# Layer 1's first buffers at the other end of SBUF beside the transform back, one pool of PSUM banks for both, the weights' sums and the first units' loads moved

## The chip, the cores and the metric

One core of a Trainium2 chip. The time is that of one execution on the device, in microseconds (us); lower is better. The kernel before runs in 5853.41 us, the median of three executions (5851.69 to 5869.86).

The engines are called by the profile's names: PE (matrix multiplications; PEld is its weight load), DVE (vector), ACT (scalar, with activation tables), POOL (GpSimd) and SP (SyncE, which here only issues DMAs). SBUF is the on-chip memory, PSUM the eight banks in which PE accumulates.

## The reference

The input x is (16, 16, 256, 256) in float32: 16 batches of 16 channels of 256 x 256 points. Two layers follow each other, each a group norm (8 groups of 2 channels in a batch), a branch and a residual sum.

```python
x = x + _L0_conv_ref(_gn(x), ty, tx, poles1, poles2, residues)
x = x + _L1_conv_ref(_gn(x), W1, b1, Wred, bred, Wspan, bspan, W2, b2, Weca)
```

Layer 0 takes a two-dimensional Fourier transform, multiplies it by a kernel given by poles and residues, and goes back: `x1` is the inverse transform and `x2` the sum over the poles, and `x1 + x2 / Nx / Ny` is added to x.

Layer 1 works on each channel as a picture of its own: a 3x3 convolution to four features with Mish; the bottom half of the rows is reduced to one channel and gives the kernel of a 3x3 involution of the top half; top and bottom are concatenated with the channels of the bottom rolled by one, a 3x3 convolution over 64 channels with Mish follows, and its mean over the picture gives a gate for each channel that multiplies the layer's input.

## The kernel before

It is one program of four stages: `layer0_forward`, `layer0_mix`, `layer0_back` and `layer1`. The change is in the last two and in the seam between them.

**The transform back (`layer0_back`, about 2262 to 2915 us).** It goes over 256 channels (16 batches of 16), four channels to a group, so 64 groups. `fetch` issues a group's loads on SP: two loads of h from `hd` in DRAM (512 KB each, e = 0 and 1), and one of x (1 MB). For each channel PE adds up `py` in a bank, alternating `iy` times h (L951) and f times `e2` (L952), and for each pair of channels it makes `pf` (L940); ACT copies `odd` and `f` to SBUF; DVE makes `o` (L962, L963); POOL adds it to x (L964); DVE takes the moments `st` (L968). For each group `norm` follows one group behind: `mv` on DVE (L976), `gn_mean` on PE (L34), four small operations on DVE, `gn_var` on PE (L42), a square root on ACT between small DVE operations (`gnr`, L46), then the normed `zb`, one half on DVE and one on POOL (L983), and two stores of `zb` to `zn` in DRAM on SP (L992). `zn` has a border of zeros; its first and last row come from a tile `zero` (memset L903, stores L905 on POOL).

The h that the first groups read was stored to `hd` by the stage before (`hd<-h`, L788, issued by POOL).

PSUM in the back: two banks for pf, four for py, one for gn_mean and gn_var together.

**Layer 1 (`layer1`, from about 2919 us).** It has 144 units, nine for each batch. A unit loads its z rows from `zn` (`load_rows`, eight loads on SP, L1115), and then does the first convolution `c` (L1144, two turns of 48 passes), Mish into `bot` (L1153) and `wide` (L1161), the reduction `pr` (L1172) to `r` (L1182), the involution `pd` (L1194, 192 passes) with `t` and `top` on DVE (L1209, L1211), and stores to `cf`. The second convolution (`c2ps`, L1272) of the batch before is interleaved. While unit i is in its involution, unit i+1's convolution stands in front of it in PE's order: c(0), pr(0), c(1), pd(0), pr(1), c(2) and so on.

Before the first unit come the loads of the weights (L58, L1066), sums of them on DVE (L1054 to L1071), `mean2` and `std2` from the norms' scalars (L1081, L1082), memsets on POOL (`zero1`, the two `wide`, borders), and the load of ACT's Mish table (`preload_act_table_set`).

**What sets the order.** In both stages the order on PE, ACT, DVE and POOL is that of the program's text inside `tc.manual_schedule`. The order on SP is set by the framework's scheduler. Tile pools hand out their buffers in turn, and a buffer's next user waits for the last reader. A pool that is opened where a closed pool lay waits for that pool's last users; this holds for all of layer 1's pools in the kernel before, since the back's pools close when `layer0_back` returns. At most eight of the DMAs that SP issues are under way at once, by the program's semaphores.

The order of the back, for each channel n:

```python
for n in range(C * nb + 5):
    if n and n % 4 == 0 and n <= C * nb:
        fetch(n // 4 + 2)
    if n < C * nb:
        channel(n)
        if n % 2 == 0:
            rows_poles(n + 2)
    if 1 <= n <= C * nb:
        moments(n - 1)
    if n and n % 4 == 0 and n <= C * nb:
        last = norm(n // 4 - 1)
    next(last, None)
```

Of the kernel before, what the change touches and what calls it, by code (L numbers as in the profile page):

```python
# [1 line left out]

# [8 lines left out]
F32 = mybir.dt.float32  # L11
# [7 lines left out]
C = 16  # L19
N = 256  # L20
# [9 lines left out]
def group_norm_scalars(nc, sm, psum, ones, mv, n, neg_mean, rstd, times=1.0):  # L30


    mean = psum.tile([P, n], F32, tag="gn", name="gn_mean")
# [7 lines left out]
    var = psum.tile([P, n], F32, tag="gn", name="gn_var")  # L41
# [30 lines left out]
def layer0_forward(ctx, tc, d, al, bd, tabs):  # L72
# [36 lines left out]
    psn = ctx.enter_context(tc.tile_pool(name="psn", bufs=1, space=PSUM))  # L109
    passing = ExitStack()  # L110
# [65 lines left out]
    def halves(b, cg, eo, mv):  # L176
# [5 lines left out]
        yield from group_norm_scalars(nc, sm, psn, ones, mv, 2, nm, rs, 4.0)  # L182
# [694 lines left out]
@with_exitstack  # L877
def layer0_back(ctx, tc, d, hd, bd, zn, mr, ed):

    nc = tc.nc
    nb = d["x"].shape[0]
    cp = ctx.enter_context(tc.tile_pool(name="bc", bufs=1))
    iy = load(nc, cp, d["iy"], [P, 2, P], "iy")
    ones = load(nc, cp, d["ones"], [P, P], "ones")


    e1 = cp.tile([P, C, N], F32, name="e1")
    e2 = cp.tile([P, C, N], F32, name="e2")  # L890
    for k in range(0, C, 4):
        for i, t in enumerate((e1, e2)):
            nc.sync.dma_start(out=t[:, k : k + 4], in_=ed[:, i, k : k + 4])

    hp = ctx.enter_context(tc.tile_pool(name="bh", bufs=4))
    fp = ctx.enter_context(tc.tile_pool(name="bf", bufs=3))
    sm = ctx.enter_context(tc.tile_pool(name="bs", bufs=3))
    psf = ctx.enter_context(tc.tile_pool(name="psf", bufs=2, space=PSUM))
    psy = ctx.enter_context(tc.tile_pool(name="psy", bufs=4, space=PSUM))
    psn = ctx.enter_context(tc.tile_pool(name="psn", bufs=1, space=PSUM))  # L900

    zero = cp.tile([nb, C * (N + 2)], F32, name="zero")
    nc.gpsimd.memset(zero, 0.0)  # L903
    for y in (0, N + 1):
        nc.gpsimd.dma_start(out=zn[:, y].rearrange("b c x -> b (c x)"), in_=zero)  # L905
    zbuf = [cp.tile([P, 2, 4, N + 2], F32, name=f"zb{i}") for i in range(3)]
    for t in zbuf:
        for x in (0, N + 1):
            nc.gpsimd.memset(t[:, :, :, x : x + 1], 0.0)

    groups, r2s, fs = {}, {}, {}

    def fetch(i):

        if i >= 4 * nb:
            return
        b, k0 = i // 4, i % 4 * 4
        if k0 == 0:
            r2s[b] = fp.tile([P, P], F32, tag="r2", name="r2")
            nc.sync.dma_start(out=r2s[b], in_=bd[b])  # L920
        h = hp.tile([P, 2, 4, N], F32, tag="h", name="h", bufs=3)
        for e in range(2):
            nc.sync.dma_start(
                out=h[:, e].rearrange("p k x -> p (k x)"),
                in_=hd[e, :, :, b % 2, b // 2, k0 : k0 + 4].rearrange("v f k x -> (v f) (k x)"),
            )
        x = hp.tile([P, 4, 2, N], F32, tag="x", name="x")
        nc.sync.dma_start(
            out=x.rearrange("p k h x -> p (k h) x"),
            in_=d["x"][b, k0 : k0 + 4].rearrange("k (h p) x -> p (k h) x", p=P),  # L930
        )
        groups[i] = h, x, sm.tile([P, 4, 6], F32, tag="st", name="st")

    def rows_poles(n):

        if n >= C * nb:
            return
        b, k = divmod(n, C)
        pf = psf.tile([P, 2, N], F32, tag="pf", name="pf")
        nc.tensor.matmul(pf, lhsT=r2s[b], rhs=e1[:, k : k + 2], start=True, stop=True)  # L940
        fs[n] = fs[n + 1] = fp.tile([P, 2, N], F32, tag="f", name="f")
        nc.scalar.copy(fs[n], pf)

    def channel(n):

        k = n % C
        h, x, _ = groups[n // 4]
        f = fs.pop(n)
        py = psy.tile([P, 2, N], F32, tag="py", name="py")
        for e in range(2):  # L950
            nc.tensor.matmul(py[:, e], lhsT=iy[:, e], rhs=h[:, e, k % 4], start=True, stop=False)  # L951
            nc.tensor.matmul(  # L952
                py[:, e],
                lhsT=f[:, k % 2, P * e : P * e + P],
                rhs=e2[:, k],
                start=False,
                stop=True,
            )
        odd = fp.tile([P, N], F32, tag="odd", name="odd")
        nc.scalar.copy(odd, py[:, 1])  # L960
        o = fp.tile([P, 2, N], F32, tag="o", name="o")
        nc.vector.tensor_tensor(o[:, 0], py[:, 0], odd, ALU.add)  # L962
        nc.vector.tensor_tensor(o[:, 1], py[:, 0], odd, ALU.subtract)  # L963
        nc.gpsimd.tensor_tensor(x[:, k % 4], x[:, k % 4], o, ALU.add)  # L964

    def moments(n):
        _, x, st = groups[n // 4]
        nc.vector.bn_stats(st[:, n % 4], x[:, n % 4].rearrange("p h x -> p (h x)"))  # L968

    def norm(i):  # L970

        b, k0 = i // 4, i % 4 * 4
        _, x, st = groups.pop(i)
        mv = sm.tile([P, 2, 2], F32, tag="mv", name="mv")
        for g in range(2):
            nc.vector.bn_aggr(mv[:, g], st[:, 2 * g : 2 * g + 2].rearrange("p c s -> p (c s)"))  # L976
        yield
        g0 = k0 // 2
        nm, rs = mr[:, b, g0 : g0 + 2, 0], mr[:, b, g0 : g0 + 2, 1]
        yield from group_norm_scalars(nc, sm, psn, ones, mv, 2, nm, rs)  # L980
        z = zbuf[i % 3]
        for g, eng in ((0, nc.vector), (1, nc.gpsimd)):
            eng.tensor_scalar(  # L983
                z[:, :, 2 * g : 2 * g + 2, 1 : N + 1],
                x[:, 2 * g : 2 * g + 2].rearrange("p k h x -> p h k x"),
                nm[:, g : g + 1],
                rs[:, g : g + 1],
                ALU.add,
                ALU.mult,
            )  # L990
        for h in range(2):
            nc.sync.dma_start(  # L992
                out=zn[b, 1 + P * h : 1 + P * h + P, k0 : k0 + 4].rearrange("p k x -> p (k x)"),
                in_=z[:, h].rearrange("p k x -> p (k x)"),
            )
        yield

    E = mybir.EngineType  # L1000
    with tc.manual_schedule(engines={E.PE, E.Activation, E.DVE, E.Pool}):
        for i in range(3):
            fetch(i)
        rows_poles(0)
        last = iter(())
        for n in range(C * nb + 5):
            if n and n % 4 == 0 and n <= C * nb:
                fetch(n // 4 + 2)
            if n < C * nb:
                channel(n)  # L1010
                if n % 2 == 0:
                    rows_poles(n + 2)
            if 1 <= n <= C * nb:
                moments(n - 1)
            if n and n % 4 == 0 and n <= C * nb:
                last = norm(n // 4 - 1)
            next(last, None)

# [3 lines left out]
def layer1(ctx, tc, d, zn, cf, mr, nb):  # L1024
# [9 lines left out]
    wp = ctx.enter_context(tc.tile_pool(name="l1w", bufs=1))  # L1034
    zp = ctx.enter_context(tc.tile_pool(name="l1z", bufs=3))
    fp = ctx.enter_context(tc.tile_pool(name="l1f", bufs=2))
    rp = ctx.enter_context(tc.tile_pool(name="l1r", bufs=3))
    op = ctx.enter_context(tc.tile_pool(name="l1o", bufs=4))
    sm = ctx.enter_context(tc.tile_pool(name="l1s", bufs=2))
# [5 lines left out]
    nc.scalar.preload_act_table_set("mish")  # L1045
# [7 lines left out]
    w02 = wp.tile([P, 2, 32], F32, name="w02")  # L1053
    nc.vector.tensor_tensor(w02, c2[:, :, 0], c2[:, :, 2], ALU.add)  # L1054
    halves = []
    for name, op_ in (("w_sum", ALU.add), ("w_difference", ALU.subtract)):
        w = wp.tile([P, 2, 32], F32, name=name)
        nc.vector.tensor_tensor(w, w02, c2[:, :, 1], op_)
        nc.vector.tensor_scalar(w, w, 0.5, None, ALU.mult)
        halves.append(w)  # L1060
    weights = [c2[:, :, 0], *halves, c2[:, :, 2]]
    w12 = wp.tile([P, 2, 32], F32, name="w12")
    nc.vector.tensor_tensor(w12, c2[:, :, 1], c2[:, :, 2], ALU.add)
    pm = load(nc, wp, d["pm"], [P, 3, C], "pm")
    weca = wp.tile([P, 3], F32, name="weca")
    nc.sync.dma_start(out=weca, in_=d["weca"].to_broadcast([P, 3]))  # L1066

    wca = wp.tile([P, C], F32, name="wca")
    nc.vector.tensor_scalar(wca, pm[:, 0], weca[:, 0:1], None, ALU.mult)
    for k in (1, 2):  # L1070
        nc.vector.scalar_tensor_tensor(  # L1071
            wca, pm[:, k], weca[:, k : k + 1], wca, ALU.mult, ALU.add
        )
# [551 lines left out]
```

## Time and profile before

| | |
|---|---|
| median of three executions | 5853.41 us (5851.69, 5853.41, 5869.86) |
| the profiled execution's own time | 5856.29 us |
| its span (first to last instruction) | 5854.5 us |
| mean granted clock of PE | 0.982 of full |
| busy share of the span | PE 93%, DVE 80%, ACT 40%, POOL 49% |
| DMA | 1370 MB, mean 234 GB/s |
| chain of waits by engine | PE 69%, DVE 17%, DMA 8%, issue 4% |
| last ph matmul of the mix, first py of the back | 2262.6 us, 2281.09 us |
| last py of the back | 2905.4 us |
| first c of layer 1, c of unit 2 | 2927.48 us, 2959.00 us |

All lines of the profile are from one execution. "x4" behind an instruction is a count. In the chain of waits each line is a start, a length and what was at work; a line "PEq" or "SPq" is the engine's queue issuing. A releaser is given as `<-` and a name. "granted clock" is the share of TensorE's full speed that the chip allowed in that stretch.

### The profile page before, as it was taken

Reading aid. Unit: us, or ns where it says so; the run is one execution under the profiler, and the core shown is the slowest. Engines: PE = TensorE matmul, PEld = TensorE weight load, DVE = VectorE, ACT = ScalarE, POOL = GpSimd, SP = SyncE. Lnnn points to the kernel's source line nnn. Section 1 sums busy time; section 2 is a strip of 40 time slices with the busy share of each in tenths; the row PEclk is TensorE's granted clock in tenths of the full one; section 3 lists DMA queues with packets and bytes.
Section 4 is the critical chain, followed back from the end, with each engine's and each line's share of the span. In section 5 each row is a group of like instructions: output and inputs, shape, how many; then the busy total and the mean of one; then the engine's idle time right before and its main releaser. Section 6 shows DMA issues by size and latency. Waiting matters only on the chain.

```text
span 5854.5 us, 216537 instructions
## 1 busy us (share of the span) xinstructions
PE 5425.1 (93%) x94280; PEld 3313.5 (57%) x94280; DVE 4664.1 (80%) x8643; ACT 2322.4 (40%) x4158; POOL 2863.9 (49%) x4090
## 2 busy tenths in 40 slices
PE   6999999788889888999899999999999999999996
PEld 5888988667767676777644343334444333434332
DVE  8888988477888886888838887878878788788784
ACT  2444556344444443222244343443434344344331
POOL 1334444433333334666643655556555566545563
PEclk9999999899999999999999999999999999999998
DMA  3455655556656667999878888999888998889887
GB/s 99 138 150 152 169 144 146 159 184 199 196 193 200 194 196 240 326 327 326 291 202 239 273 261 257 281 286 286 268 256 275 285 295 274 257 262 278 277 282 234
DMA packets 814470, 1370.07 MB, mean 234 GB/s; under 512 B 139824, under 2 KB 629168, under 8 KB 798384
## 3 DMA queue, kind: packets, MB, share of 16 engines
q1 hardware_dynamic: 596176, 881.61, 48.1%
q0 software_dynamic: 217344, 474.61, 26.2%
q8 instruction: 740, 12.12, 0.9%
q14 instruction: 210, 1.72, 0.1%
HBM read 729.78 MB, written 556.47 MB: 220 GB/s over the span
## 4 chain that ended last, share of the span: by engine, by line
PE 69%; DVE 17%; DMA 8%; issue 4%; ACT 1%; POOL 1%; SPq 0%; DVEq 0%; ACTq 0%; POOLq 0%
PE pd L1194 17%; PE c2ps L1272 15%; PE c L1144 13%; DMA z<-in_x 5%; PE ph L760 4%; PE ps L706 4%; PE pg L725 3%; PE pr L1172 3%; PE py L951 2%; PE py L952 2%; PE pt L741 2%; DVE st L167 2%; DVE zb L983 1%; DVE st L968 1%; PE px L306 1%
## 5 line engine op out<-in xcount | busy, mean ns | idle before, releaser
L1263 DVE TENSOR_TENSOR planes<-rows 128x1152 f32<-128x1152 f32 x960 | 1180.3, 1291 | 4.3 <-PE c2ps L1272 4.3
L1224 POOL DMA_DIRECT2D cf<-top x1152 | 667.6, 686 | 900.5 <-DVE top L1211 739.5
L1194 PE MATMUL pd<-wide,dw 32*32 32x512 f32 x27648 | 990.5, 598 | 30.2 <-issue 29.8
L1144 PE MATMUL c<-z,w 18*64 18x512 f32 x13824 | 800.3, 595 | 16.3 <-DMA z<-zn 16.3
L1194 PEld LDWEIGHTS pd<-wide,dw 32*32 32x32 f32 x27648 | 539.0, 103 | 465.6 <-issue 183.3
L1209 DVE TENSOR_TENSOR t<-pd,r 128x512 f32<-128x512 f32 x576 | 357.5, 682 | 353.9 <-PE pd L1194 353.2
L1144 PEld LDWEIGHTS c<-z,w 18*64 18x64 f32 x13824 | 320.2, 131 | 489.3 <-issue 348.6
L1242 POOL DMA_DIRECT2D cf<-bot x720 | 384.7, 582 | 347.1 <-DMA cf<-top 156.3
L780 POOL TENSOR_TENSOR h<-w 128x256 f32<-128x256 f32 x258 | 210.1, 814 | 586.3 <-DVE w L774 583.4
L1272 PE MATMUL c2ps<-planes,c 128*32 128x512 f32 x3968 | 454.4, 592 | 1.8 <-DVE planes L1313 1.8
L1211 DVE TENSOR_TENSOR top<-pd,t 128x512 f32<-128x512 f32 x576 | 357.4, 682 | 120.6 <-PE pd L1194 120.6
L1362 POOL TENSOR_SCALAR o<-o,scale,mean 128x258 f32<-128x258 f32 x488 | 421.0, 871 | 58.5 <-DVE scale L1354 44.9
L1153 ACT ACTIVATE bot<-c,b 128x512 f32<-128x512 f32 x576 | 365.0, 684 | 165.0 <-issue 123.1
L964 POOL TENSOR_TENSOR x<-x,o 128x512 f32<-128x512 f32 x256 | 324.5, 1268 | 215.0 <-DVE o L963 215.0
L205 PE MATMUL pu<-fy,f 128*128 128x128 f32 x2048 | 411.7, 283 | 0.0
L212 PE MATMUL pv<-at,f 128*128 128x128 f32 x2048 | 400.4, 278 | 0.0
L322 POOL DMA_DIRECT2D al<-o x544 | 338.0, 628 | 113.9 <-ACT o L313 77.4
L1298 ACT COPY mid<-c2ps 128x512 f32<-128x512 f32 x120 | 70.5, 588 | 807.2 <-PE c2ps L1272 807.2
L1161 ACT ACTIVATE wide<-c,b 128x512 f32<-128x512 f32 x576 | 365.1, 693 | 0.0
L725 PE MATMUL pg<-alb,s 128*32 128x64 f32 x16896 | 288.0, 221 | 73.9 <-issue 55.7
L706 PE MATMUL ps<-tt,lt 64*32 64x256 f32 x8448 | 292.4, 388 | 57.4 <-issue 24.6
L951 PE MATMUL py<-h,iy 128*128 128x256 f32 x1024 | 316.4, 391 | 10.1 <-DMA h<-hd 10.1
(244 smaller groups left out, 10146.8 us busy)
## 6 DMA issues: line engine op xcount, KB each, us to landing
rows<-cf SPq DMA_DIRECT2D x128, 2176.0 KB
cf<-top POOLq DMA_DIRECT2D x896, 112.0 KB, 6.8
cf<-bot POOLq DMA_DIRECT2D x336, 224.0 KB, 6.7
z<-zn SPq DMA_DIRECT2D x576, 129.0 KB
alb<-alx SPq DMA_DIRECT2D x132, 512.0 KB
zn<-zb SPq DMA_DIRECT2D x128, 516.0 KB
o<-zn SPq DMA_DIRECT2D x128, 516.0 KB
z<-in_x SPq DMA_DIRECT2D x64, 1024.0 KB
```

The source lines that it names most:

```text
L205: nc.tensor.matmul(pu[:, h, :, :, e].rearrange("p v g m -> p (v g) m"), lhsT=f[:, e, c, h], rhs=fy[:, e].rearrange("p (n m) -> p n m", m=2 ...
L212: nc.tensor.matmul(pv[:, a, h], lhsT=f[:, e, c, h], rhs=at[:, e, 4 * cg + c].rearrange("p l m -> p (l m)"), start=e == 0, stop=e == 1,)
L706: nc.tensor.matmul(ps[32 * g : 32 * g + 32, odd, v], lhsT=lt[lanes, kk, g, 1 - v : 3 - v].rearrange("p l c -> p (l c)"), rhs=tt[lanes, kk, g],
L725: nc.tensor.matmul(ps[32 * q : 32 * q + 32, x], lhsT=s[:, i].rearrange("p v k -> p (v k)"), rhs=alb[:, :, column(i)], start=True, stop=True,)
L951: nc.tensor.matmul(py[:, e], lhsT=iy[:, e], rhs=h[:, e, k % 4], start=True, stop=False)
L1144: nc.tensor.matmul(ps[half, a][to : to + 64], lhsT=w1[lanes, dx], rhs=self.z[lanes, c : c + 2, dx : dx + N], start=dx == 0, stop=dx == 2,)
L1194: nc.tensor.matmul(out[32 * k : 32 * k + 32], lhsT=dw[lanes, kernel, dx], rhs=self.feat[lanes, 2 * k : 2 * k + 2, dx : dx + N], start=dx == 0,
L1224: nc.gpsimd.dma_start(out=rows[y + 2 * lo : y + 2 * hi, :, c + 2 * k : c + 2 * k + 2].rearrange("y f c x -> y f (c x)"), in_=o[32 * k + 2 ...
L1242: nc.gpsimd.dma_start(out=rows[y + 4 * lo : y + 4 * hi, to : to + n].rearrange("p c x -> p (c x)"), in_=src.rearrange("p c q x -> p (c q x)"),
L1263: nc.vector.tensor_tensor(planes[:, k, rows], x[:, rows], y[:, rows], op_)
L1272: nc.tensor.matmul(ps[32 * j : 32 * j + 32], lhsT=w[:, blk], rhs=src[:, 4 * j + blk : 4 * j + blk + 4], start=(i, blk) == (0, 0), stop=(i, ...
L1362: eng.tensor_scalar(o[:, i], o[:, i], scale[:, c + i : c + i + 1], mean2[:, b, c + i : c + i + 1], ALU.mult, ALU.add,)
```

## The change

- `layer0_back` becomes a generator that is run inside `layer1`. It takes its banks from layer 1's pool of eight (`bank`), for pf, py, gn_mean and gn_var alike. It yields at channel 32, at channel 48 and behind the last channel's passes.
- The pools `l1w` (weights, and the first `wide`), `l1z` (z) and a new one `l1b` (bot) lie at the right end of SBUF, beside the back's pools. The others of layer 1 (`l1f` with r and top, and so on) and a new pool `l1l` (the second `wide`, mean2, std2, planes and others) are opened when the back is done.
- At channel 32 unit 0's z rows are loaded, at channel 48 unit 1's (both are in batch 0, which the back has stored by then).
- Behind the last channel's passes the first half of unit 0's convolution is put into PE's order, ahead of the last norm's gn_mean and gn_var; its activations (`mish`) come behind the back in the program's text.
- The weights' sums, mean2 and std2 and the preload of the Mish table stand in the text behind the back, outside of the handwritten order.
- The tile `zero` for the border rows of `zn` is 16 x 258 instead of 16 x 4128, and is stored with a broadcast over the batches.

In the order of instructions that results, compared engine by engine with the kernel before: SP issues h(0, e=1), x(0), h(0, e=0) where it issued h(0, e=0), h(0, e=1), x(0); the last two stores to `hd` stand ahead of the work on `zero`; the loads of w1, b1, wr and dw stand behind x(3), the other small loads and unit 0's z behind x(10); the nine DVE operations on weights stand around channel 39; the memset of `wide0` at channel 17; and ACT has three table loads at the second seam where it had one: Mish for unit 0's first half, the square root for the last norm, Mish again.

```diff
+def layer0_back(tc, d, hd, bd, zn, mr, ed, bank):
...
-    zero = cp.tile([nb, C * (N + 2)], F32, name="zero")
+        zero = cp.tile([C, N + 2], F32, name="zero")
...
-        nc.gpsimd.dma_start(out=zn[:, y].rearrange("b c x -> b (c x)"), in_=zero)
+            nc.gpsimd.dma_start(
+                out=zn[:, y].rearrange("b c x -> c b x"),
+                in_=zero.unsqueeze(1).to_broadcast([C, nb, N + 2]),
+            )
...
-        pf = psf.tile([P, 2, N], F32, tag="pf", name="pf")
+            pf = bank([2, N], "pf")
...
-        py = psy.tile([P, 2, N], F32, tag="py", name="py")
+            py = bank([2, N], "py")
...
                 if n < C * nb:
                     channel(n)
                     if n % 2 == 0:
                         rows_poles(n + 2)
+                if n in (2 * C, 3 * C, C * nb - 1):
+                    yield
                 if 1 <= n <= C * nb:
                     moments(n - 1)
...
-    wp = ctx.enter_context(tc.tile_pool(name="l1w", bufs=1))
-    zp = ctx.enter_context(tc.tile_pool(name="l1z", bufs=3))
-    fp = ctx.enter_context(tc.tile_pool(name="l1f", bufs=2))
+    wp = ctx.enter_context(tc.tile_pool(name="l1w", bufs=1, side="right"))
+    zp = ctx.enter_context(tc.tile_pool(name="l1z", bufs=3, side="right"))
+    bp = ctx.enter_context(tc.tile_pool(name="l1b", bufs=2, side="right"))
...
-    nc.scalar.preload_act_table_set("mish")
+    transform = back(bank)
+    next(transform)
...
+    begin_unit(0)
+    next(transform)
+    begin_unit(1)
+    next(transform)
+    begun = units[0].convolution(0)
+    for _ in transform:
+        pass
+
+    fp = ctx.enter_context(tc.tile_pool(name="l1f", bufs=2))
...
+    lp = ctx.enter_context(tc.tile_pool(name="l1l", bufs=1))
+    nc.scalar.preload_act_table_set("mish")
+    w02 = wp.tile([P, 2, 32], F32, name="w02")
+    nc.vector.tensor_tensor(w02, c2[:, :, 0], c2[:, :, 2], ALU.add)
...
     with tc.manual_schedule(engines={E.PE, E.Activation, E.DVE, E.Pool}):
-        begin_unit(0)
-        begin_unit(1)
         u = units[0]
-        u.convolve(0)
+        u.mish(0, begun)
         u.convolve(1)
         u.reduce()
...
-    layer0_back(tc, d, hd, bd, zn, mr, tabs[2])
-    layer1(tc, d, zn, cf, mr, nb)
+    layer1(tc, d, zn, cf, mr, nb, partial(layer0_back, tc, d, hd, bd, zn, mr, tabs[2]))
```

## The prediction

> **What bounds the kernel now.** I read the page first (PE busy 93% of the span, the chain of waits 69% PE), then cut the span into stages with the windows view. Its columns are the stretch, the busy time of PE, PEld, DVE, ACT and POOL with instruction counts, the granted clock, the DMA share and GB/s.
>
> ```profile
> 2255.00:2285.00 30.00, 12.13 (x195) 9.01 (x192) 5.75 (x14) 3.12 (x8) 11.54 (x19) 0.69 0.84 303
> 2400.00:2800.00 400.00, 383.73 (x1646) 296.19 (x1645) 352.40 (x987) 117.48 (x287) 272.97 (x206) 1.00 0.94 327
> 2900.00:2930.00 30.00, 8.41 (x30) 4.89 (x28) 15.73 (x48) 1.52 (x5) 13.63 (x17) 0.63 0.63 197
> 2930.00:2960.00 30.00, 30.00 (x436) 12.63 (x442) 4.49 (x8) 13.27 (x21) 3.58 (x7) 0.74 0.42 107
> 4000.00:5000.00 1000.00, 992.89 (x18398) 403.95 (x18394) 824.19 (x1057) 406.80 (x739) 577.17 (x895) 1.00 0.90 279
> ```
>
> The transform back and layer 1 are both limited by PE (96% and 99% busy). Between them PE works 8.4 of 30 us and then runs at a reduced clock; before the back it idles too. Only these two seams and additions to PE's steady path can matter. The chain of waits across the second seam (start, length, work):
>
> ```profile
> 2910.63 0.60 PE gn_var L42 x2
> ...
> 2912.74 1.61 DVE zb L983
> ...
> 2914.76 4.16 DMA zn<-zb
> 2919.07 0.35 SPq L58
> ...
> 2924.23 3.20 DMA z<-zn
> 2927.48 3.55 PE c L1144 x4
> 2931.03 11.66 PE c L1144 x92
> 2942.69 2.69 PE pr L1172 x16
> 2945.38 5.45 PE c L1144 x96
> 2950.83 7.15 PE pd L1194 x178
> 2957.98 1.02 PE pr L1172 x16
> 2959.00 5.71 PE c L1144 x96
> ```
>
> The last py ends at 2905.4. The weights and z wait for the last store to land, because layer 1's buffers lie over the back's; SP then issues ten loads before z. Unit 0's 96 passes cost 15.2 us where unit 1's cost 5.45: the clock is half until 2945.2. Unit 2's first pass is at 2959.00, 53.6 us after the last py. From there units follow each other with PE busy throughout, so a lead at this point is kept to the end.
>
> The first seam, same view, and then ACT's table load and three pairs of h loads on SP from the timeline (start, duration, line, work):
>
> ```profile
> 2262.71 3.53 POOL zero L903
> ...
> 2267.41 6.88 DMA hd<-h
> 2274.34 6.62 DMA h<-hd
> 2280.96 0.14 issue
> 2281.09 1.19 PE py L951 x2
> ```
>
> ```profile
> 2936.07 1.28 ACT L1153 ACT_TABLE_LOAD   x1 [24.43 <-DMA z<-zn]
> ```
>
> ```profile
> 2274.34 0.84 SPq L923 DMA_DIRECT2D h<-hd  x2
> 2280.13 4.58 SPq L923 DMA_DIRECT2D h<-hd  x2
> 2375.46 1.99 SPq L923 DMA_DIRECT2D h<-hd  x2
> ```
>
> **Part 1, the first seam: +4.2 us.** In the new instruction order the final hd stores stand ahead of the small zero's work. The zero memset shrinks from 3.53 us to the class of the 128x128 memset (0.20 us), so the last store leaves POOL about 1.5 us earlier. But SP no longer issues h(0, e=0), h(0, e=1), x(0). It issues h(0, e=1), then x(0), then h(0, e=0), which is the one that waits for the last store and the one PE's first py reads. From 2266 to 2300 the windows of 2 us show a DMA share of 0.97 to 1.05 at 360 to 405 GB/s: the transfers are a saturated line, so starting 1.5 us earlier buys nothing, and 0.52 MB of h and 1.05 MB of x now stand in front of the wanted half. 1.57 MB at 377 GB/s is 4.2 us. Bounds: -1.5 if the order on the line did not matter, +5 if stores are also late. I take 4.2 since the row 6.62 us for a 0.5 MB load (1.4 us alone) shows that loads do queue. Behind it nothing gives the time back: PE is 96% busy for the 64 groups.
>
> **Part 2, the steady back: +1.5 us.** One pool of eight banks hands out exactly eight per group (four py, two pf, gn_mean, gn_var), so each py and pf bank returns after the same distance as before, and order and waits on PE, ACT and DVE are those of before. The 9.73 us per group stays. What is new inside:
> - SP issues five weight loads behind x(3); five small loads and eight z loads behind x(10); eight z loads at channel 48. Each small issue costs 0.4 us, and a pair of h loads held up by transfers in flight took 4.58 us instead of 0.84. An h pair issued at 2375.46 is needed by the group that starts at 2392.3 and by SP's rows lands near 2383, so some 9 us hide one such delay of 4 to 5 us and the 5.2 us of 13 issues. Price 0; without that cover up to 10 us a batch.
> - The weights' sums stand in DVE's order not behind the back but around channel 39, seven of them inside one norm's chain. In the timeline of before the nine took 2923.41 to 2926.3, with 0.65 us of waiting, so 2.2 us. DVE is 88% busy and gn_var's users, then PE, wait for it: 1.0 to 2.2 us, 4 if their loads are late (they should land some 2 us ahead). I take 1.3.
> - POOL's memset of wide0 (1.87 us in its row) at channel 17: POOL is 68% busy; 0 to 0.6, I take 0.2.
>
> **Part 3, the second seam: -26.4 us.** The z tiles and weights are there long before; PE goes from the last py straight into half of unit 0's convolution, then the last norm's two matmuls, then the rest. Step by step, all passes at the full clock (5.45 us per 96):
> - 2905.4 to 2908.2: 48 passes under the DVE chain, which now runs unchanged to gn_mean at 2909.4 and gn_var at 2910.6 to 2911.2. Waiting: 3.0.
> - Second 48 passes to 2914.0. Meanwhile ACT loads the Mish table, does the first half's four activations (0.63 each in overlap), reloads for the square root, does gnr (1.5 us later than 2911.44) and loads Mish again: 3 loads of 1.28 where there was one. ACT is ready at 2914.4, bot is done and pr runs 2915.1 to 2916.1. Waiting: 1.1.
> - Unit 1's first half is clean. Its second half needs banks that the r activations free, and r lies in a buffer over the back's, so it waits for the last zn store: zb 1.5 us later, store 4.16, landed 2920.6, r done 2921.9. Unit 1's passes end at 2924.4 instead of 2921.6. Waiting: 2.8.
> - pd 7.15, pr 1.02: unit 2 at 2932.6 instead of 2959.00, 26.4 us gained. PE's bare work is 20.1 us, so 33.5 is the most that can be gained.
>
> [...] The row here shows 1.28, and its next activation at 2937.37, 0.02 us after; no run here has shown a switch back to the square root yet.
>
> **Sum.** On the profiled run's own 5856.3 us (span 5854.5 and 1.8 around it): +4.2 +1.5 -26.4 gives 5835.6. That run was 2.9 above the median of 5853.4, so 5832.7 is forecast, say 5833. A measurement of this kernel tells 0.3% (17.6 us) from no change: below 5835.8 is faster, above 5871.0 slower. The sum lies only 3 us past the line.
>
> **Rivals.**
> 1. The clock falls in the gap at 2908.2. For: in the trace the clock dropped 2.7 us after the last py and 3.8 us after the last ph (2262.6 to 2266.4), and here about 3 us hold only two tiny matmuls. Against: those two matmuls cut the gap into pieces of 1.2 us. Price: passes take 127 ns (11.66/92) instead of 57 until about 17.7 us after they resume, as between 2927.5 and 2945.2; unit 2 comes near 2939, gain 20 (17 to 22), time 5839: within 0.3%. [...]
> 2. The order of the first loads costs nothing, because the transfers are spread and e=0 overtakes. For: the last store leaves 1.5 us earlier. Against: the saturated line. Time 5833-4.2 = 5828.5.
> 3. Slower: SP jams. If the 13 and 8 loads are each held for transfers in flight as the pair at 2280.13 was, two rounds of 6.6 to 6.9 us (rows hd<-h, h<-hd) pass before the next h. That decides from the point where h lands after its group begins: beyond 9 us of slack. Two stalls of 13, and x and zn behind them delaying the next groups by as much again, cost 30 to 50 us against 20.7 of net gain: 5863 to 5883, around 5873. Against: z loads are 129 KB, a quarter of an h load.
> 4. The change does not do what it says: the sums are already "in" rather than "behind"; if the loads of c2, pm and weca land late, DVE stops with everything behind it. Priced above: +4 at most, 5836.
>
> **How the numbers follow.** The sum as it stands 0.55, of which 0.42 ends below the line and 0.13 above, since its 3 us are less than the spread of parts 1 and 2; rival 2 0.15; rival 1 with the late loads of rival 4 0.20; rival 3 0.10, two thirds of it beyond +0.3%. Faster 0.60, same 0.33, slower 0.07. The range runs from 5824 (front free, waits of part 3 some 4 us shorter) to 5845 (halved clock, front +5, sums +4); only the jam and a remnant lie outside.
>
> **What would show it.** First py near 2285 with h(0, e=0) as its releaser; 9.73 us per group after; one longer group at channel 39; last py near 2911; c directly behind it; three ACT_TABLE_LOADs within 8 us; r waiting for zn<-zb; unit 2 some 27 us after the last py instead of 53.6. Wrong would be: h loads as releasers of py in the middle of the back; clock below 1.00 behind the last py; a unit cadence in layer 1 other than before.

## The result, and the profile after

The changed kernel takes 5825.12 us (median of 7, 5813.94 to 5839.32) against 5853.41 us (median of 7, 5840.34 to 5869.86): the ratio is 0.9958 with a 95% interval of 0.9942 to 0.9974. The forecast was 5833 in a range from 5824 to 5845.

Single executions of one kernel lie up to 30 us apart, so I read the change from stages of the profiled ones, marked by events that both kernels have: the last ph matmul, the first py, the last py, and unit 2's first c.

| stage, us | before | before, again | after | after, again | forecast of the difference |
|---|---|---|---|---|---|
| last ph to first py ("first wait") | 18.5 | 19.3 | 23.7 | 24.5 | +4.2 |
| first py to last py ("back") | 624.3 | 624.3 | 625.9 | 625.1 | +1.5 |
| last py to unit 2's c ("seam") | 53.6 | 52.9 | 27.4 | 27.5 | -26.4 |
| the three together | 696.3 | 696.4 | 677.0 | 677.0 | -20.7 |
| start to last ph | 2262.6 | 2273.5 | 2257.1 | 2267.3 | 0 |
| unit 2's c to the end | 2895.6 | 2884.9 | 2898.4 | 2875.3 | 0 |

The three stages that the change touches agree within 1 us between two executions of one kernel and together gained 19.4 us. The two long stages around them moved by 10 and more in executions of the same kernel.

The seam of the changed kernel, in the chain of waits (start, length, work):

```profile
2910.75 0.40 PE gn_mean L35 x2
...
2911.86 0.35 PE gn_var L43 x2
2912.22 4.21 PE c L1103 x48
2916.43 3.19 PE pr L1138 x16
2919.62 7.00 PE c L1103 x96
2926.62 6.53 PE pd L1160 x177
2933.15 1.02 PE pr L1138 x16
2934.17 5.65 PE c L1103 x96
```

The last py ends at 2906.7 and the first 48 passes follow at once. DMA is gone from the chain. But 48 passes take 4.21 us, where the first 48 took 2.8, and pr 3.19 where it takes 1.02 in the next unit (its weight loads also wait 1.0 us for ACT's Mish into `bot`). The windows view shows the clock (the figure behind POOL's busy time; the bounds go in steps of 3.41 us from 2913.39, where the trace's record has the clock fall):

```profile
2906.57:2909.98 3.41, 2.89 (x49) 0.94 (x48) 3.31 (x9) 0.85 (x2) 2.20 (x3) 1.00 0.01 2
2909.98:2913.39 3.41, 1.91 (x28) 1.18 (x36) 1.39 (x8) 3.38 (x6) 0.94 (x1) 1.00 0.48 195
2913.39:2916.80 3.41, 3.41 (x34) 0.81 (x20) 1.47 (x5) 3.03 (x4) 1.12 (x1) 0.50 0.50 163
2916.80:2920.21 3.41, 3.41 (x24) 0.71 (x28) 2.74 (x4) 2.01 (x4) 3.35 (x9) 0.50 0.57 231
```

PE was busy for 1.91 of 3.41 us around the last norm, and the clock was half for the next two stretches, although PE was then busy throughout. It came back at 2920.21, in the stretch in which pr ran.

The table loads, in ACT's timeline:

```profile
2909.50 1.28 ACT L1119 ACT_TABLE_LOAD   x1 [2.34 <-PE c L1103]
2910.80 1.27 ACT L1119 ACTIVATE bot<-c,b 128x512 f32<-128x512 f32 x2
...
2913.24 1.28 ACT L47 ACT_TABLE_LOAD   x1
2914.53 0.20 ACT L47 ACTIVATE gnr<-gnv 128x2 f32<-128x2 f32 x1
2914.75 1.28 ACT L1119 ACT_TABLE_LOAD   x1
```

Each of the three takes 1.28 us. Behind the first two the next activation starts 0.01 to 0.02 us later; behind the third ACT waited 0.35 us for c.

The first wait, SP's timeline, and then one line of the chain of waits:

```profile
2267.18 0.38 SPq L926 DMA_DIRECT2D h<-hd  x1
2267.60 0.45 SPq L931 DMA_DIRECT2D x<-in_x  x1
2268.47 5.57 SPq L926 DMA_DIRECT2D h<-hd  x3
```

```profile
2268.47 12.29 DMA h<-hd
```

The load that the first py needs is issued third and lands 12.29 us later; before it landed 6.62 us after its issue.

### The profile page after: what moved, and what is told of

It reads as the page before. It is cut to its first block, busy times and chain, and to the rows that moved or that the text cites. A ratio compares the mean times of both kernels' runs of the same rounds, so it can differ in the third digit from the quotient of the medians.

```text
span 5832.5 us, 216530 instructions
## 1 busy us (share of the span) xinstructions
PE 5422.8 (93%) x94280; PEld 3313.2 (57%) x94280; DVE 4666.6 (80%) x8643; ACT 2324.5 (40%) x4160; POOL 2866.9 (49%) x4090
## 4 chain that ended last, share of the span: by engine, by line
PE 61%; DVE 7%; issue 2%; DMA 2%; ACT 1%; POOL 0%; SPq 0%; DVEq 0%; ACTq 0%; POOLq 0%
PE pd L1160 17%; PE c2ps L1238 15%; PE c L1103 13%; PE ph L765 3%; PE pr L1138 3%; PE ps L711 2%; PE py L954 2%; PE pg L730 2%; PE py L955 2%; DVE zb L986 1%; DVE st L971 1%; PE pt L746 1%; PE pf L943 1%; DVE o L966 1%; DVE alx L661 1%
```

## The experiments

All are edits of the changed kernel unless said otherwise, and are read by the stages above.

**The kernel before, once more.** No edit.

> The kernel before once more, to see how much each stage moves by itself from one execution to the next. Stages: last ph matmul to first py (18.5 us before, 23.7 after), first py to last py (624.3 and 625.9), last py to unit 2's first c (53.6 and 27.4), from there to the end (2895.6 and 2898.4), and everything ahead of the last ph (2262.6 and 2257.1). Theory: the change made the first stage 5.2 us longer, the second 1.6 longer and the third 26.2 shorter, while the 5.5 us ahead of the last ph and the 2.8 us in layer 1 are scatter; so this run has 18 to 19, 624 to 625 and 53 to 54, but differs by several us in the first and last part. Rival: layer 1 really became slower; then its last part is within 0.5 us of 2895.6.

Measured: 19.3, 624.3 and 52.9 us, and 2273.5 and 2884.9 in the long stages, 10.9 more and 10.7 less than the first time. The first wait and the seam miss the expected 18 to 19 and 53 to 54 by 0.3 and 0.1. The 2.8 us in layer 1 is within the scatter, and the three stages are a fit measure to about 1 us.

**The order of the first loads.** Each load of the first group is pinned behind the one before it on SP:

```diff
+            keep = tc.keep_in_program_order if i == 0 else (lambda load_: load_)
             for e in range(2):
-                nc.sync.dma_start(out=h[:, e]..., in_=hd[e, ...])
+                keep(nc.sync.dma_start(out=h[:, e]..., in_=hd[e, ...]))
...
-            nc.sync.dma_start(out=x..., in_=d["x"]...)
+            keep(nc.sync.dma_start(out=x..., in_=d["x"]...))
```

> The changed kernel with the order of SP's first loads pinned to h(0, e=0), h(0, e=1), x(0) as before. Theory (the load order costs the first wait, 1.57 MB on a full line): last ph to first py falls from 23.7 us to about 18 (17 to 19.5), and the seam behind stays at 27. Rival (the order costs nothing, and the wait is longer because the run's transfers were late): it stays between 22 and 25. Rival 2 (the small zero brings the stores forward by 2 us and the time with it): 16.5.

Measured: first wait 19.6 us. The load's line in the chain of waits is now

```profile
2283.90 8.09 DMA h<-hd
```

The order costs 4 to 5 us, as the theory has it, and the small zero returns nothing: the wait stays a little over that of before. The bound of 19.5 was missed by 0.1.

**Without the early half convolution.** `begun` is gone and unit 0 convolves behind the last norm:

```diff
-    begun = units[0].convolution(0)
...
-        u.mish(0, begun)
+        u.convolve(0)
```

> The changed kernel with the first half of unit 0's convolution behind the last norm's two matmuls (its early start undone, buffers and loads as in the change). Theory (most of the seam's gain is that z and weights no longer wait for the last store; the early half brings only its own passes, about 3 us, and what it saves in clock): last py to unit 2's c 29 to 36 us against 27.4 with it and 53.6 before; the clock falls, since PE stands for about 5 us, and comes back late, so nearer 36. Rival (the early half is what matters): 40 us or more.

Measured: 33.4 us, the back 624.7. In the chain of waits unit 0's convolution runs whole at half clock (the trace's record has 17.07 us of it, from 3.2 us after the last py on):

```profile
2908.14 10.47 PE c L1103 x96
2918.61 3.24 PE pr L1138 x16
```

The clock was back at 2922.57, again at the end of a stretch of 3.41 us with pr in it. So of the 26 us gained in the seam, 20 are left without the early half; they come from the rest of the change, above all from z and weights that no longer wait for the last store. The early half brings 6: 2.8 us of its passes, which ran at the full clock, and the rest, as I read it (not tested by itself), from fewer passes at half clock.

**The sums really behind.** All nine DVE operations stand behind the last norm; three of them are pinned, and the others came behind them too:

```diff
-    nc.vector.tensor_tensor(w02, c2[:, :, 0], c2[:, :, 2], ALU.add)
+    keep = tc.keep_in_program_order
+    keep(nc.vector.tensor_tensor(w02, c2[:, :, 0], c2[:, :, 2], ALU.add))
...
-    nc.vector.tensor_tensor(w12, c2[:, :, 1], c2[:, :, 2], ALU.add)
+    keep(nc.vector.tensor_tensor(w12, c2[:, :, 1], c2[:, :, 2], ALU.add))
...
-    nc.vector.tensor_scalar(wca, pm[:, 0], weca[:, 0:1], None, ALU.mult)
+    keep(nc.vector.tensor_scalar(wca, pm[:, 0], weca[:, 0:1], None, ALU.mult))
```

> The changed kernel with the nine DVE operations on the weights pinned behind the last norm. Theory (they cost the one long group, 10.99 us instead of 9.74, and nothing behind the back, where DVE waits 9.5 us for pd): the ninth interval between norms falls to 9.7, the back to 624.6 (624.2 to 625.0), the seam stays within 0.5 us of 27.4. Rival (the long group comes from z loads delaying h): it stays at 11.

Measured: the ninth interval falls from 10.99 to the usual 9.74, the back is 624.5, the seam 27.4. The sums cost 1.25 us, by standing inside a norm's chain; in the changed kernel's DVE timeline they come between gnv and gnr:

```profile
2378.23 0.85 DVE L1369 TENSOR_TENSOR w<-c 128x64 f32<-128x64 f32 x1
...
2379.28 0.15 DVE L48 RECIPROCAL gnr<-gnr 128x2 f32<-128x2 f32 x1
```

The back fell by less than that difference because the fifteenth interval was 10.64 here (10.13 in the changed kernel, 9.74 in its repeat). That is the second batch of z loads, next.

**The two batches of loads together.** Unit 1's z loads come at channel 33:

```diff
-                if n in (2 * C, 3 * C, C * nb - 1):
+                if n in (2 * C, 2 * C + 1, C * nb - 1):
```

> The changed kernel with unit 1's eight z loads right behind unit 0's, at channel 33 instead of 48, so that the two batches of loads meet. In the changed kernel the second batch held SP's queue for 12.1 us, and one interval between norms (the fifteenth) was 0.4 us longer than 9.74; the first batch held it 7.1 us. Theory (the cover of about 9 us is nearly used up by one batch; two in a row run past it): SP is held 18 to 25 us, loads of h, x or r2 come 5 to 12 us late, and the back grows from 625.9 to 630 to 638. Rival (the loads are small and the cover holds): the back stays within 625 to 627.

Measured: the back took 627.0 us; two intervals were 1.0 us longer and the fifteenth was as usual. SP's timeline shows the sixteen loads, and below it the changed kernel's second eight, with the line of its chain of waits that they delayed:

```profile
2374.01 12.95 SPq L1073 DMA_DIRECT2D z<-zn  x16
```

```profile
2408.30 12.11 SPq L1073 DMA_DIRECT2D z<-zn  x8
```

```profile
2425.63 10.55 DMA r<-bd
```

The theory's sizes were wrong: sixteen loads held SP for 12.95 us and not 18 to 25, and the delay was 2 us and not 5 to 12. The rival's bound holds. But the cover is not ample: in the changed kernel the r2 load of the next batch of the back came 0.5 us late for PE's pf. The mechanism of the jam is there, at well under 1 us.

**PE kept busy.** Matmuls into unused columns of the gn banks, six ahead of gn_mean and three ahead of gn_var, in the last norm alone:

```diff
+    def busy(name, more):
+        if spare is None:
+            return bank([n], name)
+        t = bank([2, N], name)
+        for _ in range(more):
+            nc.tensor.matmul(t[:, 1], lhsT=ones, rhs=spare, start=True, stop=True)
+        return t[:, 0, :n]
...
-    mean = bank([n], "gn_mean")
+    mean = busy("gn_mean", 6)
...
-    var = bank([n], "gn_var")
+    var = busy("gn_var", 3)
```

> The changed kernel with nine idle matmuls (128x256 into unused columns of the gn banks): six ahead of the last gn_mean, three ahead of the last gn_var, so that PE does not stand while the last norm's scalars are made. They add nothing to the result. In the changed kernel the clock was half for 6.83 us there, the second half of unit 0's convolution took 4.2 us and unit 1's 7.0. Theory (the halved clock is mostly hidden behind the wait of r for the last store): the clock stays full, the 48 passes take 2.8 us, but r still ends near 17 us after the last py, so last py to unit 2's c falls only from 27.4 to 26.6 (26.0 to 27.0). Rival (the clock is the seam's loss): it falls by the 3 us and more that the slow passes cost, to 24.5 or less. Rival 2 (the clock falls all the same): 27 to 29.

Measured: 32.9 us. None of the three. The clock stayed full through the norm, and 48 passes took 2.8 us. But nine were too many (they held gn_mean up by 1.3 us, and with it the last store), PE stood 2.0 us for r at 17 us, and there the clock fell for 10.24 us: the last 40 passes took 6.0. A wait elsewhere gave back more than the cure had won.

**r at the other end.**

```diff
-            self.r = fp.tile([P, 2, 4, H], F32, tag="r", name="r")
+            self.r = bp.tile([P, 2, 4, H], F32, tag="r", name="r")
```

> The changed kernel with r in the pool at SBUF's other end, so that unit 0's relu no longer waits for the last store to zn. Theory: with the clock at half until about 13.5 us after the last py, unit 1's passes are the limit, and last py to unit 2's c falls from 27.4 to 26.2 (25.5 to 26.8). Rival (r's wait is off the path because the slow clock hides it): within 0.4 of 27.4.

Measured: 28.0 us, outside the theory's range and outside the rival's bound. The clock was half for 10.24 us here, where it was 6.83 in the changed kernel. The run of the load order, with r where it was, also had 10.24 us and a seam of 28.2. Against that run moving r brings 0.1 us, which is the rival's reading: r's wait lies under the slow clock.

**Both.** The nine matmuls, and r moved.

> Both: the nine idle matmuls and r at the other end. Theory (clock and r's wait cover each other, so that only both together pay): last py to unit 2's c 24.2 (23.5 to 25.0), more below 27.4 than the two single gains (0.8 and 1.2) add up to. Rival (they add up): 25.4 or more. The forecast's sum with r's wait of 2.8 us taken away would give 24.4.

Measured: 28.0 us. The clock stayed full, and unit 1's passes ended 17.6 us after the last py, 2.3 us earlier than in the changed kernel. Then PE stood 1.3 us for a Mish into the second `wide`, whose memset on POOL waited for the last store, as r had:

```profile
2919.51 1.82 POOL L1396 MEMSET wide<- 128x2064 f32 x1 [6.62 <-DMA zn<-zb]
```

pd began again 19.9 us after the last py. Neither theory had this wait; the rival's 25.4 or more is met, but not for its reason.

**The last square root first.** The first Mish is pinned behind gnr, so that ACT loads one table:

```diff
-    nc.scalar.preload_act_table_set("mish")
+    tc.keep_in_program_order(nc.scalar.preload_act_table_set("mish"))
...
-                nc.scalar.activation(self.bot[:, c : c + 2], ...)
+                keep(nc.scalar.activation(self.bot[:, c : c + 2], ...))
```

> The changed kernel with the last norm's square root pinned ahead of unit 0's first Mish, so that ACT has one table load at the seam instead of three. Theory (the two added loads lie beside other work; moving the Mish back holds the banks of the second half): last zn store about 2 us earlier, but the second half waits for banks until 2 us later and PE stands longer, so the clock is half for longer; last py to unit 2's c 29 to 32 against 27.4. Rival (the table loads and their waits are on the path): 26.1 or less, by 1.3 us a load.

Measured: 28.0 us, with the clock half for 10.24 us. Against the runs of 28.0 and 28.2 with the same stretch at half clock it is the same. gnr came 1.9 us earlier after the last py and nothing came of it. So in this seam, with the clock half, one table load instead of three gains nothing on balance (the first Mish came later for it); the theory's loss of 2 us or more was wrong too.

**Three matmuls, r and the second wide moved.**

```diff
-    mean = busy("gn_mean", 6)
+    mean = busy("gn_mean", 2)
...
-    var = busy("gn_var", 3)
+    var = busy("gn_var", 1)
...
-    wide.append(lp.tile([P, 8, N + 2], F32, name="wide1"))
+    wide.append(wp.tile([P, 8, N + 2], F32, name="wide1"))
```

> The changed kernel with three idle matmuls (two ahead of the last gn_mean, one ahead of the last gn_var; nine were too many, they held gn_mean up by 1.4 us), r at SBUF's other end, and the second wide there too, since with r moved pd stood 1.3 us for the memset of that wide. Theory: pr then follows ACT's third table load, unit 1's passes run at the full clock and end 17 us after the last py, unit 2's c comes at 25.3 (24.8 to 26.0) against 27.4. Rival (the clock falls in the gaps that are left, of 0.3 us): 27 to 29.

**All that paid.** The same, with the pinned first loads and the pinned sums.

> All that paid in one kernel: first loads in the order of before, the weights' sums pinned behind the back, three idle matmuls, r and the second wide at SBUF's other end. Against the changed kernel's stages (first wait 23.7, back 625.9, seam 27.4, together 677.0; before 696.4): 19.3, 624.6, 25.3, together 669.2 (667 to 671). Time: 27 us under before, a ratio of 0.9954 (0.993 to 0.997 with the scatter of the stages that the change does not touch). Rival: gains in the front are taken back at the second batch of z loads: together 673 or more.

Measured together: the first has a seam of 27.4 us, with the clock half for 6.83 us; the second 24.5, with the clock full until unit 2. Their seams differ only by the nine sums on DVE, which in their own run left the seam at 27.4. The second half of unit 0's convolution, from PE's timeline of the one and of the other:

```profile
2922.15 4.53 PE L1113 MATMUL c<-z,w 18*64 18x512 f32 x46
```

```profile
2907.44 2.82 PE L1114 MATMUL c<-z,w 18*64 18x512 f32 x46
```

So two such stretches at half clock cost 2.9 us between these two, and three matmuls keep the clock in one execution and not in the other. With the clock full, ACT's table loads stand in the chain of waits, where in the changed kernel there were none of them:

```profile
2907.76 1.28 ACT L56
...
2909.27 1.28 ACT L1130
...
2911.31 1.63 PE pr L1149 x12
```

They are the loads for the square root and for Mish again. What they would give back with the clock full was not tested. All stages of the last version: 19.8, 624.3, 24.5, together 668.6, as expected (667 to 671), 8.4 less than the changed kernel. Its time is 5819.83 us (median of 6), a ratio to before of 0.9946 (0.9924 to 0.9967).

**The changed kernel once more, beside it.**

> The changed kernel once more, beside the one above and the kernel before on the same chip. Theory: its stages are 23.7, 625.5, 27.4 to 28.2, as in the variants that share them, so it is 19 to 20 us under before and 7 to 9 us over the kernel above: ratio 0.9967 (0.995 to 0.9985). Rival: the gain is larger than the three stages show, as the 28 us between the medians says; then the ratio is 0.995 or less.

Measured: the stages in the table above, and 5824.95 us (median of 6) against 5859.53 us for the kernel before in these rounds (median of 11), a ratio of 0.9944 (0.9928 to 0.9961). The two intervals overlap, so by time the last version is not shown to be faster than the changed kernel, only by its stages. The theory's ratio (0.995 to 0.9985) is missed and the rival's condition is met: the gain by time is larger than the 19.4 us of the stages.

## Why the prediction was right, point by point

- **First wait, +4.2:** it was +5.2 in the first pair of profiles and +5.2 in the second. The mechanism is shown by the run that puts the order back, which returns 4.1 to 4.9 us; so rival 2 (the order costs nothing) is out, and 0.3 to 1.1 us are not explained. The windows of 2 us read 0.97 to 1.10 at 342 to 422 GB/s, somewhat wider than the working has it; its 377 lies inside. One sentence of the working and of the section on the change was wrong: the last two stores to `hd` do not stand ahead of the small zero's work, they stand behind all of it (in the kernel before one of them stood ahead of its second store). They are still 2 us earlier: the last is issued 4.5 us after zero's memset begins instead of 6.5. As forecast, that bought nothing; the wanted h was issued 11.4 us after the last ph instead of 11.7, and the chain of waits has an e load (e<-ed, landed at 2268.38) ahead of it.
- **Back, +1.5:** +1.6, and +0.8 in the repeat. The sums' 1.3 is shown (1.25). Loads were priced at 0 behind a cover of 9 us; they cost 0 to 0.9 us at the fifteenth interval. The 0.2 for wide0's memset does not show: the memset ran at 2365.14 us, behind the sums of 33 channels and not at channel 17, and the interval that holds it has the usual 9.74. 0.3 us at the fifty-fourth interval is in every version of the change and not explained. From the first py to the first gn_mean, where the clock comes back, the fourteen profiles took 14.5 to 16.0 us (15.9 and 15.7 before, 15.3 and 15.0 after), so that +1.6 came this close to +1.5 is partly luck.
- **Seam, -26.4:** -26.2, and -25.4 in the second pair, but by another way. The forecast took the full clock and charged waits for the norm (3.0), ACT (1.1) and r (2.8). Measured from the last py, gn_var ended at 5.5 as forecast (5.8). But the clock fell, and the second half ended at 9.7 instead of 8.6 and pr at 12.9 instead of 10.7. r was done at 17.1 instead of 16.5, and unit 1's passes came to their end at about the forecast place (19.9 by its profile, 19.0 forecast), since the slow passes ran in the time that was charged for r. pd then took 6.53 instead of 7.15, and unit 2 came at 27.4 where the working has 27.2. That the number agrees is in part luck: a cost that the sum left out lay under one that it charged.
- **Rival 1, the halved clock, came true,** in all seven profiles that have the early half and no idle matmuls, and in one of the two with three. The prediction had named a clock below 1.00 behind the last py as a sign of being wrong, and in this step it was. Against it I had said that two tiny matmuls cut the gap; the clock fell nevertheless. The seam reached the forecast's number all the same, because rival 1's price of 6 us was too high. Its step was "until about 17.7 us after they resume", a time taken from the kernel before. The runs show no such time: in the eleven profiles with a half clock ahead of pr it came back at the end of the stretch of 3.41 us in which most of the sixteen matmuls of pr ran, and never in the passes of c before it, whether those took 4 us or 10. In the kernel before c's 96 passes stood ahead of pr, here 48. Its 127 ns a pass, and the 15.2 us that the working puts down to the clock alone, also hold a wait: in the kernel before PE waited for further z rows up to 2932.16 us, six passes in 4.7 us, and the other 90 took 10.5 us, 117 ns each. The last two versions show a price of 2.9 us for two stretches, with r and the second wide out of the way.
- **Table loads:** the working charges 1.28 us a load, and no run had shown a switch back to the square root by then. Here the load for the square root starts 0.02 us behind the activation before it and gnr follows it by 0.01 us, so nothing beyond the row's 1.28 is seen. The run with one load instead of three has the same seam; in the last version, with the clock full, two of the loads are in the chain.
- **Rival 3, the jam,** exists and cost under 1 us, or 2 us where the two batches meet. Rival 4 held in its first half (the sums are inside the back) and not in its second (their loads were not late).
- **What stays open:** the median of 5825 lies inside the range, but nearly 8 us under 5833, while the stages gained 1.3 us less than the 20.7 forecast. Medians fell by 28 and 35 us, the stages by 19.4. The interval of the first ratio (15 to 34 us) holds that, that of the second (23 to 42 us) does not. The rest would have to lie ahead of the last ph or in layer 1. In the twelve profiles of the changed kernel and its variants these took 2252 to 2273 us and 2875 to 2899 us (means 2261.5 and 2888.8), in the two of before 2262.6 and 2273.5, and 2895.6 and 2884.9. The means are 6.5 and 1.4 us lower with the change; whether it moves them by some us can't be told from two.

## What to carry to other kernels

Cut a profile into stages by events that both kernels share, and judge each stage by itself: here three stages resolved 1 us in a program whose time scatters by up to 30. In the first wait 1.57 MB ahead of the half that the first py needed, with the DMA share at 0.97 to 1.10, cost 4.1 to 4.9 us, so look at which transfer the first reader needs and keep that in front. Where one wait lies under another (a slow clock, a buffer, a memset), taking away one alone can show nothing (r's move by itself brought 0.1 us); take them away together (with r, the second wide and three matmuls the last version's seam is 2.9 us shorter), and expect the next one (here the second wide, 1.3 us, and then ACT's table loads, 1.28 us each).

## What the runs showed of the hardware

- **The clock's states last multiples of 3.41 us** in these traces: half for 3.41, 6.83, 13.65, 17.07, 20.48, 23.89 and 37.55 us in those of the kernel before and of the changed one, apart from the last state, which ends with the trace, and for 10.24 us in four of the variants. A stretch with PE busy for 1.91 of 3.41 us (2909.98 to 2913.39 in the changed kernel) was followed by half clock. The busy time as the profile has it doesn't decide alone: 2.74 us kept the clock in the repeat, 2.85 us or more lost it in unit 2 of the last version (PE stood 0.56 us in all from 2927 to 2957), 3.17 us (with two passes of c that waited) lost it in the run with three idle matmuls, and 2.11 us kept it in the run with nine and r moved.
- **Passes of 18 rows did not bring the clock back** in these traces: in the kernel before it stayed half through three whole stretches of c's passes (2931.97 to 2942.21 us), in the run without the early half through 10.5 us of them, and returned with pr (64*32 in the trace) or, in the run with nine idle matmuls, with pd. At the first seam, where py is 128*128, it was back 5.8 us after the first py in the kernel before and 4.5 in the changed one, and 3.1 to 6.1 us after it in all fourteen profiles. What in these matmuls makes the difference was not tested, and a stretch of c's passes alone at the full clock did not lose it (2920.21 to 2923.62 us in the changed kernel).
- **The seam's length went with where the stretches lay.** With the early half and no idle matmuls the fall came 4.1 to 5.1 us after the last py, for three stretches (seam 28.0 to 28.5), or 6.7 to 6.9 us after it, for two (27.4 to 27.5).
